# A two-layer graph network on one core: forward transforms by even and odd halves of the nodes on 64 by 64 tiles

## The chip, the core and the metric

The kernel runs on one core of a Trainium2 chip. The metric is the device time of one execution in microseconds (us); smaller is better. The engines are TensorE (PE in the profile, with PEld for its weight loads), VectorE (DVE), ScalarE (ACT), GpSimd (POOL) and SyncE (SP), which issues most of the DMAs. All data are fp32; an fp32 matmul appears in the trace as two records.

## The reference

The input holds 128 graphs of 128 nodes with 256 features. Layer 0 is a gated unit whose inputs are a convolution along the nodes and a message product; layer 1 is a graph convolution over five groups of nodes, cut here, since the change leaves it alone.

```python
h = relu(layernorm(x))                               # (128, 128, 256)
# layer 0, on h seen as 16 sequences of 2048 nodes elsewhere; here by graph
c = relu(bn1(conv1(h)))                              # 256 -> 256, one tap
c = bn2(conv2(c))                                    # 256 -> 256, 17 taps along the nodes, padding 8
x_conv = relu(c + h)
s = h @ w_se.T + b_se
A = exp(-dist(s)) * adj
x_nmp = A @ relu(h @ w_msg.T + b_msg)
z, r, n = gates([x_conv, x_nmp] @ w_ih.T, h @ w_hh.T)
x = x + (1 - z) * n + z * h
# layer 1
x = x + fused_graph_convs(relu(layernorm(x)))
```

conv2 is the part that matters here. Its 17 taps run along the 128 nodes of each graph.

## The kernel before

conv2 is computed in the frequency domain. With padding a graph's row of nodes has length 136 (LW), which gives 68 frequency pairs (NP_). Three stages follow one another.

**Heads.** The 128 graphs are worked in 32 blocks of four (BB). For each block: `head_load` fetches x by node (L196 on, tile ln), `head_stats` takes mean and variance on DVE (L204, L205, L208) and their power of -0.5 on POOL (L210), `head_norm` normalises on DVE (L223; the first blocks on ACT, L220), `head_turn` transposes on PE (L233) into two banks of PSUM, one for each half c of the features, and ACT writes them out with a relu (L234, tile ht), which SP stores to DRAM (htd, L235) for the gates. `head_conv1` multiplies by conv1's weights (L247), two graphs in a bank; DVE adds the shift of the batch norm (L250, tile h) and ACT takes the relu in place (`head_relu`, L254). `head_spectra` transforms along the nodes: for each half c and two graphs, a bank receives two matmuls with the 128 by 136 matrix fd (L263). The first two graphs' bank is copied to the spectra X by ACT (L273), the other's by DVE (L271), so the two engines read different banks. X is held in two tiles, X0 with 20 frequency pairs and X1 with 48, so each copy is two instructions of 80 and 192 columns.

Between these, `weight_spectra` (L176) transforms conv2's taps: four row tiles of 17 rows each write four banks; three of them are copied by ACT (L185), the fourth by DVE (L183), in two parts of the taps of three columns and a last of two that ACT copies alone. Each finished piece goes to DRAM (vd). Their operands w2 are loaded three buffers deep.

The engines keep the order in which the program is written in this stage. `heads` runs over i: conv1 of block i, first half; a piece of weight spectra; the relu; half of the statistics of block i+3; conv1, second half; the turn of block i+1; the relu; the norm of block i+2; on odd i another piece of weight spectra; the transforms of block i-1; the other half of the statistics. The work of one odd and one even i is called a pair of blocks below.

PSUM has eight banks, and `bank()` hands them out in a fixed cycle, each as a tile of its own:

```python
banks[1] = (n + 1) % 8
return pool.tile([P, 512], F32, tag=f"bank{n}", name="bank")
```

**Spectral products.** `spectral` takes one frequency pair after another: it loads the weight spectra v (four pairs at a time, SP), forms s = -2a - d on DVE (L334) from the two parts a and d of X, forms vs = vr + vi on POOL (L337, two instructions), multiplies by three groups of four matmuls (L340, L345), copies one product by ACT (L342), adds it on DVE (L346) and stores the result y.

**Gates and layer 1.** `load_h` loads ht again for each block, the inverse transform brings y back to nodes, and the message product, the gates and the second layer follow. The constants of the transforms are made on the host in `_spectral_constants`.

Of the kernel before, what the change touches and what calls it, by code (L numbers as in the profile page):

```python
# [75 lines left out]
def gnn_kernel(ctx: ExitStack, tc: tile.TileContext, io, out0: bass.AP, out1: bass.AP):  # L76
# [11 lines left out]
    turns = ExitStack()  # L88
    banks = [turns.enter_context(tc.tile_pool(name="turns", bufs=1, space=bass.MemoryType.PSUM)), 0]

    def bank():
        pool, n = banks
        if n is None:
            return pool.tile([P, 512], F32, tag="bank", name="bank")
        banks[1] = (n + 1) % 8
        return pool.tile([P, 512], F32, tag=f"bank{n}", name="bank")

# [6 lines left out]
    vec = cst.tile([P, NV], F32)  # L104
    fd = hc.tile([P, LW], F32)
    wc1 = hc.tile([P, C, D], F32)
# [6 lines left out]
    bnr = hc.tile([P, 2, D], F32)  # L113
    sh1 = bnr[:, 1, :]
    brz = cst.tile([P, 4], F32)

    def constant_loads():
        nc.sync.dma_start(wc1, io["wc1"].rearrange("(c p) o -> p c o", p=P))
        nc.sync.dma_start(fd, io["fd"])

    def constants():


        def scales(j, v0):
            g, b, m, v = (vec[:, v0 + 2 * q:v0 + 2 * q + 2] for q in range(4))
            sc, sh = bn[:, j, 0, :], bn[:, j, 1, :]
            ve = cst.tile([P, C], F32, name=f"bnve{j}")
            nc.vector.tensor_scalar(ve, v, EPS, None, op0=ALU.add)
            rs = cst.tile([P, C], F32, name=f"bnrs{j}")
            nc.gpsimd.tensor_tensor(rs, ve, mhalf[:, :C], op=ALU.pow)  # L130
            nc.vector.tensor_mul(sc, g, rs)
            nc.vector.tensor_mul(ve, m, sc)
            nc.vector.tensor_sub(sh, b, ve)

        scales(0, V_BN1)
        bnb = hc.tile([P, 2 * C, P], F32, name="bnb")
# [52 lines left out]

    xs, stats, hcs, h1s = {}, {}, {}, {}  # L190

# [20 lines left out]

    def head_norm(i, wk=None):
        mv, rs = stats.pop(i)
# [22 lines left out]

    def head_conv1(wk, i, h):
        if not h:
            h1s[i] = wk.tile([P, BB, D], F32, tag="h1", name="h1", bufs=2)  # L240
        ht = hcs[i]
        ps = bank()
        pv = ps.rearrange("p (b d) -> p b d", b=2)
        for bb in range(2):
            b = 2 * h + bb
            for c in range(C):
                nc.tensor.matmul(pv[:, bb, :], ht[:, c, b * N:(b + 1) * N], wc1[:, c, :],  # L247
                                 start=c == 0, stop=c == C - 1)
        hv = h1s[i][:, 2 * h:2 * h + 2, :]
        nc.vector.tensor_tensor(hv, pv, sh1[:, None, :].to_broadcast([P, 2, D]), op=ALU.add)  # L250

    def head_relu(i, h):
        hv = h1s[i][:, 2 * h:2 * h + 2, :]
        nc.scalar.activation(hv, hv, AF.Relu)  # L254

    def head_spectra(X, i):
        h1 = h1s.pop(i)
        g0 = i * BB
        for c in range(C):
            for h in range(BB // 2):  # L260
                ps = bank()
                for bb in range(2):
                    nc.tensor.matmul(ps[:, bb * LW:(bb + 1) * LW], h1[:, 2 * h + bb, c * P:(c + 1) * P], fd,  # L263
                                     start=True, stop=True)
                s = ps[:, :2 * LW].rearrange("p (g d) -> p d g", g=2)
                d0 = 0
                for xt in X:
                    xv = xt[:, c].rearrange("p a k g -> p (a k) g")
                    dst, d1 = xv[:, :, g0 + 2 * h:g0 + 2 * h + 2], d0 + 2 * xt.shape[2]
                    if h:  # L270
                        nc.vector.tensor_copy(dst, s[:, d0:d1])  # L271
                    else:
                        nc.scalar.copy(dst, s[:, d0:d1])  # L273
                    d0 = d1

    def heads(wk, xk, ahead, X, between, consts):

        for i in range(NBLK + 1):
            if i + ahead < NBLK:
                head_load(xk, ahead, i + ahead, nc.sync)  # L280
            if i < NBLK:
                head_conv1(wk, i, 0)
            between()
            if i < NBLK:
                head_relu(i, 0)
            if i == 0:
# [7 lines left out]
            if i < NBLK:  # L294
                head_relu(i, 1)
# [15 lines left out]
    def spectral(bp, X, p_from, p_to, amid):  # L311

        x, base = X
        for p in range(p_from, p_to):
# [66 lines left out]
    with front as es:  # L381
# [9 lines left out]
        with ExitStack() as ws:  # L391
# [20 lines left out]
            def some_spectra(k=1):  # L412
                for _ in range(k):
                    if not spectra and todo:
                        spectra.append(weight_spectra(wp, *todo.pop(0), taps.pop(0)))
                    if spectra and next(spectra[0], STOP) is STOP:
                        spectra.pop(0)
                        if len(todo) > 2:
                            taps.append(taps_load(wp, *todo[2], nc.sync))
                        some_spectra()  # L420
# [6 lines left out]
            nc.sync.dma_start(fw, row("fw", 5))  # L427
            taps.append(taps_load(wp, *todo[2], nc.sync))
            consts = constants()
            head_stats(hk, 0)  # L430
# [11 lines left out]
            some_spectra()  # L442
            heads(hk, xk, ahead, X, some_spectra, consts)
            while spectra or todo:
                some_spectra()
        turns.close()
        banks[:] = [ctx.enter_context(tc.tile_pool(name="psum", bufs=8, space=bass.MemoryType.PSUM, reuse_waits="tile")), None]

# [697 lines left out]


def _spectral_constants():

# [4 lines left out]
    def rows(t):  # L1154

        t = np.asarray(t)
        c = np.cos(2 * np.pi * np.outer(np.arange(NP_ + 1), t) / LW)
        s = np.sin(2 * np.pi * np.outer(np.arange(NP_ + 1), t) / LW)
        return c, s

    gt = np.zeros((P, NP_, 2))
    fd = np.zeros((P, NP_, 2))
    inv = np.zeros((NP_, 2, P))
    c, s = rows(np.arange(KW))
    for r in range(4):
        k = slice(32 * r, 32 * r + KW)
        gt[k, 0, 0], gt[k, 0, 1] = c[0], c[NP_]
        gt[k, 1:, 0], gt[k, 1:, 1] = c[f].T, s[f].T
    c, s = rows(np.arange(P) + PAD)
    fd[:, 0, 0], fd[:, 0, 1] = c[0], c[NP_]  # L1170
    fd[:, 1:, 0], fd[:, 1:, 1] = c[f].T, (-s[f] - c[f]).T
    c, s = rows(np.arange(P))
    inv[0, 0], inv[0, 1] = c[0] / LW, c[NP_] / LW
# [5 lines left out]
    d = {"gt": gt.reshape(P, LW), "fd": fd.reshape(P, LW), "idm": inv[:P], "idr": idr.reshape(P, 2 * P)}  # L1179
    return {k: np.ascontiguousarray(v, dtype=np.float32) for k, v in d.items()}  # L1180


def _lay_out(a):
# [10 lines left out]
    by = (-1, BB, P)  # L1194
    d = {"x": cc(a["x"].reshape(*by, 2 * P).transpose(0, 2, 1, 3)), "xT": cc(a["x"].reshape(-1, BB * P, 2, P).transpose(0, 3, 2, 1)), "adjT": cc(a["adj"].reshape(*by, P).transpose(0, 3, 1, 2))}
    d["vec"] = cc(np.concatenate(
# [72 lines left out]
```

## Time and profile before

| | us |
|---|---|
| median of three runs | 1842.88 (1842.33 to 1843.74) |
| the profiled execution, its own time | 1843.16 |
| its span in the trace | 1841.2 |
| heads (to the last PE work before the products) | 0 to 259.7 |
| spectral products | 262.8 to 437 |
| gates and layer 1 | 437 to the end |

The profile is of one execution. A line of a group names the source line, the engine, the operation, output and inputs with shapes and count, and after the bar the busy time, the mean duration in ns and the idle time of the engine ahead of these instructions with what ended it. The chain of waits is the sequence of work that ended last, followed back from the end. The table of windows gives busy time of each engine in a stretch; the granted clock is a share of full speed, and DMA the mean busy share of the 16 DMA engines.

### The profile page before, as it was taken

Reading aid. Unit: us, or ns where it says so; the run is one execution under the profiler, and the core shown is the slowest. Engines: PE = TensorE matmul, PEld = TensorE weight load, DVE = VectorE, ACT = ScalarE, POOL = GpSimd, SP = SyncE. Lnnn points to the kernel's source line nnn. Section 1 sums busy time; section 2 is a strip of 40 time slices with the busy share of each in tenths; the row PEclk is TensorE's granted clock in tenths of the full one; section 3 lists DMA queues with packets and bytes.
Section 4 is the critical chain, followed back from the end, with each engine's and each line's share of the span. In section 5 each row is a group of like instructions: output and inputs, shape, how many; then the busy total and the mean of one; then the engine's idle time right before and its main releaser. Section 6 shows DMA issues by size and latency. Waiting matters only on the chain.

```text
span 1841.2 us, 31324 instructions
## 1 busy us (share of the span) xinstructions
PE 1823.7 (99%) x11016; PEld 1587.0 (86%) x11016; DVE 1323.1 (72%) x3290; ACT 736.9 (40%) x1630; POOL 648.5 (35%) x803
## 2 busy tenths in 40 slices
PE   9999999999999999999999999999999999999998
PEld 7888888887888888888788888888788888888786
DVE  6888855556887887878665788878656677877553
ACT  6666641112443343333334433433343433343343
POOL 1111125675435443544221354344313234443100
PEclk9999999999999999999999999999999999999999
DMA  8888889996633333334234433333333533242134
GB/s 303 319 315 317 306 293 309 351 322 227 170 76 84 73 90 83 85 77 115 71 103 110 123 85 76 78 82 111 88 83 89 135 80 92 73 97 58 35 91 130
DMA packets 217904, 267.26 MB, mean 145 GB/s; under 512 B 104822, under 2 KB 181323, under 8 KB 215699
## 3 DMA queue, kind: packets, MB, share of 16 engines
q1 hardware_dynamic: 212563, 247.32, 45.2%
q10 hardware_dynamic: 5184, 17.93, 2.4%
q8 instruction: 88, 1.44, 0.3%
q14 instruction: 69, 0.57, 0.1%
HBM read 168.84 MB, written 96.35 MB: 144 GB/s over the span
## 4 chain that ended last, share of the span: by engine, by line
PE 92%; DMA 3%; DVE 2%; SPq 1%; POOL 1%; ACT 1%; issue 0%; DVEq 0%; POOLq 0%; ACTq 0%
PE bank L686 44%; PE bank L345 6%; PE bank L247 6%; PE bank L1013 5%; PE bank L954 5%; PE bank L587 5%; PE bank L340 3%; PE bank L263 3%; PE bank L637 3%; PE bank L566 3%; PE bank L176 2%; PE bank L233 1%; PE bank L933 1%; PE bank L863 1%; DMA nt<-in_adjN_dram 1%; PE bank L543 1%
## 5 line engine op out<-in xcount | busy, mean ns | idle before, releaser
L686 PE MATMUL bank<-t,sw 128*128 128x256 f32 x1152 | 291.8, 380 | 1.0 <-POOL t L661 0.4
L699 POOL TENSOR_TENSOR u<-u,m 128x256 f32<-128x256 f32 x128 | 93.7, 732 | 462.6 <-ACT m L697 413.9
L686 PEld LDWEIGHTS bank<-t,sw 128*128 128x128 f32 x1152 | 214.7, 190 | 34.0 <-issue 3.0
L686 PE MATMUL bank<-t,wih 128*128 128x256 f32 x768 | 200.2, 383 | 0.0
L686 PEld LDWEIGHTS bank<-t,wih 128*128 128x128 f32 x768 | 143.1, 190 | 29.3 <-DVE o L726 6.6
L337 POOL TENSOR_TENSOR vs<-v 128x256 f32<-128x256 f32 x134 | 98.7, 762 | 72.4 <-DMA v<-vd 48.6
L247 PE MATMUL bank<-wc,ht 128*128 128x256 f32 x512 | 124.0, 386 | 0.0
L686 PE MATMUL bank<-xc,wih 128*128 128x256 f32 x384 | 115.4, 382 | 1.6 <-ACT xc L570 1.6
L686 PE MATMUL bank<-xn,wih 128*128 128x256 f32 x384 | 115.1, 382 | 0.0
L686 PE MATMUL bank<-t,whh 128*128 128x256 f32 x384 | 114.6, 380 | 0.1
L1013 PE MATMUL bank<-w,hh 128*125 128x256 f32 (+9 forms) x480 | 113.6, 380 | 0.1
L686 PE MATMUL bank<-ht,whh 128*128 128x256 f32 x384 | 110.5, 381 | 0.5 <-DVE msg L606 0.4
L610 ACT ACTIVATE msg<-msg 128x512 f32<-128x512 f32 x64 | 36.8, 622 | 183.1 <-DVE msg L606 183.1
L570 ACT ACTIVATE xc<-xc,bn 128x512 f32<-128x512 f32 x64 | 46.2, 722 | 152.1 <-DVE xc L569 152.1
L210 POOL TENSOR_TENSOR rs<-ve,mhalf 128x4 f32<-128x4 f32 x32 | 32.3, 1009 | 207.5 <-DVE ve L208 201.2
L247 PEld LDWEIGHTS bank<-wc,ht 128*128 128x128 f32 x512 | 92.4, 190 | 14.2
L1013 PEld LDWEIGHTS bank<-w,hh 128*125 128x125 f32 (+9 forms) x480 | 84.4, 178 | 18.1 <-DVE hh L959 1.2
L185 ACT COPY sp<-bank 128x408 f32<-128x408 f32 (+1 forms) x160 | 66.8, 509 | 71.6 <-PE bank L176 71.6
L954 PE MATMUL bank<-ax,w 128*128 128x500 f32 (+9 forms) x352 | 94.4, 404 | 1.1 <-DVE xc L569 1.1
L334 DVE SCALAR_TENSOR_TENSOR s<-X 128x256 f32<-128x256 f32 x67 | 44.0, 659 | 66.4 <-PE bank L345 66.4
L704 DVE TENSOR_TENSOR u<-bank,u 128x256 f32<-128x256 f32 x128 | 53.4, 417 | 49.2 <-PE bank L686 48.6
L342 ACT COPY k<-bank 128x256 f32<-128x256 f32 x67 | 25.0, 373 | 145.9 <-PE bank L340 145.9
(214 smaller groups left out, 4423.8 us busy)
## 6 DMA issues: line engine op xcount, KB each, us to landing
vd<-sp SPq DMA_DIRECT2D x16, 2176.0 KB
v<-vd SPq DMA_DIRECT2D x34, 1024.0 KB
w<-in_w_dram SPq DMA_DIRECT2D x40, 512.0 KB
ln<-in_x_dram SPq DMA_DIRECT2D x32, 512.0 KB
htd<-ht SPq DMA_DIRECT2D x32, 512.0 KB
yd<-ys ACTq DMA_DIRECT2D x32, 512.0 KB
ht<-htd SPq DMA_DIRECT2D x32, 512.0 KB
ym<-yd SPq DMA_DIRECT2D x32, 512.0 KB
```

The costliest lines, as they stand in the source:

```text
L185: nc.scalar.copy(dst, s)
L247: nc.tensor.matmul(pv[:, bb, :], ht[:, c, b * N:(b + 1) * N], wc1[:, c, :], start=c == 0, stop=c == C - 1)
L263: nc.tensor.matmul(ps[:, bb * LW:(bb + 1) * LW], h1[:, 2 * h + bb, c * P:(c + 1) * P], fd, start=True, stop=True)
L337: nc.gpsimd.tensor_tensor(vs[:, c], vr[c], vi[c], op=ALU.add)
L340: nc.tensor.matmul(p1[:, :D], a[:, c], vs[:, c], start=c == 0, stop=c == C - 1)
L345: nc.tensor.matmul(ps[:, k * D:(k + 1) * D], u[:, c], w[c], start=c == 0, stop=c == C - 1)
L566: nc.tensor.matmul(ps[:, b * N:(b + 1) * N], ym[:, 2 * h + b, o * P:(o + 1) * P], idm, start=False, stop=b == 1)
L587: nc.tensor.matmul(ps[:, b, :], d[:, b * N:(b + 1) * N], w, start=True, stop=True)
L686: nc.tensor.matmul(ps, w, d, start=n == 0, stop=n == len(pairs) - 1)
L699: nc.gpsimd.tensor_tensor(got["u4"], got["u2"], got["m5"], op=ALU.add)
L954: nc.tensor.matmul(pv[:, q - q0, :], w1s[k5 + g][:, c, q * P:(q + 1) * P], xv[:, c], start=c == 0, stop=c == C - 1)
L1013: nc.tensor.matmul(ps[:n1, :D], hh[:, q, at:at + n1], w2s[k5 + g][:, q, :], start=q == 0, stop=q == HID // P - 1)
```

## The change

Nodes are put in an order in which the second 64 are mirrored: `_order()` reverses them, on the host, in x, in both dimensions of adj, and in the output. A block of x is laid out so that a tile's partitions hold the first halves of two graphs and its neighbour the mirrored second halves. Sum and difference of a node and its mirror then suffice: cosines act on the sums, sines on the differences, each with 64 nodes and 68 frequencies. `fd` becomes three 68-column parts: cosines, sines, and the sums of the cosines.

In the heads:

- `head_conv1` writes h = max(conv1, -shift) on DVE in place of the add, and the relu on ACT goes; the shift enters again as a constant (`shk`) when the spectra are written.
- `head_sums` forms sum and difference of the two halves on POOL, two instructions of 256 columns for each half of a block.
- `head_spectra` issues, for each half c of the features, 16 matmuls of 64 by 64 by 68 on four tiles into two banks; the two row tiles (one graph each) write one bank each; ACT copies the odd parts and DVE adds `shk` to the even parts, each of them from both banks, again in 80 and 192 columns.
- `bank()` hands out two-bank tiles; a bank is one half of such a tile.
- The norm of block i+2 is three instructions on ACT and one on POOL in place of four on DVE.
- On even i the transforms of block i-1 stand right behind the weight spectra, ahead of conv1's second half; on odd i they stay where they were.

In the products DVE forms s = d - a and d = d + a as two operations in place of one, POOL subtracts in place of adding. `load_h` puts ht back in the order of graphs by two DMAs in place of one. w2 has two buffers, `bnb` moves to another pool, and the constants of the inverse transform change on the host, not in size.

```diff
@@ bank
-        banks[1] = (n + 1) % 8
-        return pool.tile([P, 512], F32, tag=f"bank{n}", name="bank")
+        if n % 2 == 0:
+            two = pool.tile([P, 2, 512], F32, tag=f"bank{n // 2}", name="bank")
+        banks[1:] = (n + 1) % 8, two
+        return two[:, n % 2, :]
+
+    def two_banks():
+        if banks[1] % 2:
+            bank()
+        bank(), bank()
+        return banks[2]
@@ constants
+        for c in range(C):
+            nc.gpsimd.tensor_scalar(shk[:, c, :], fd[:, 2, :], bn[:, 0, 1, c:c + 1], -2.0, op0=ALU.mult, op1=ALU.mult)
@@ taps_load
-        w2 = pool.tile([P, WCH // 4, P], F32, tag="w2", name="w2", bufs=3)
+        w2 = pool.tile([P, WCH // 4, P], F32, tag="w2", name="w2", bufs=2)
@@ head_norm
-            if wk is not None:
+            if wk is not None and (b < BB - 1 or last is None):
                 nc.scalar.activation(xs[i][:, b, :], xs[i][:, b, :], AF.Identity, bias=nm[:, b:b + 1],
                                      scale=rs[:, b:b + 1])
                 continue
-            nc.vector.tensor_scalar(xs[i][:, b, :], xs[i][:, b, :], mv[:, b, 0:1], rs[:, b:b + 1],
-                                    op0=ALU.subtract, op1=ALU.mult)
+            (last or nc.vector).tensor_scalar(xs[i][:, b, :], xs[i][:, b, :], mv[:, b, 0:1], rs[:, b:b + 1],
+                                              op0=ALU.subtract, op1=ALU.mult)
@@ head_conv1, head_relu, head_sums
-        nc.vector.tensor_tensor(hv, pv, sh1[:, None, :].to_broadcast([P, 2, D]), op=ALU.add)
-
-    def head_relu(i, h):
-        hv = h1s[i][:, 2 * h:2 * h + 2, :]
-        nc.scalar.activation(hv, hv, AF.Relu)
+        nc.vector.tensor_tensor(hv, pv, nsh1[:, None, :].to_broadcast([P, 2, D]), op=ALU.max)
+
+    def head_sums(ep, i, h):
+        if not h:
+            evens[i] = ep.tile([P, 2, D], F32, tag="ev", name="ev", bufs=2)
+        lo, hi = h1s[i][:, 2 * h, :], h1s[i][:, 2 * h + 1, :]
+        nc.gpsimd.tensor_tensor(evens[i][:, h, :], hi, lo, op=ALU.add)
+        nc.gpsimd.tensor_tensor(hi, hi, lo, op=ALU.subtract)
@@ head_spectra
         for c in range(C):
+            ps = two_banks()
             for h in range(BB // 2):
-                ps = bank()
-                for bb in range(2):
-                    nc.tensor.matmul(ps[:, bb * LW:(bb + 1) * LW], h1[:, 2 * h + bb, c * P:(c + 1) * P], fd,
-                                     start=True, stop=True)
-                s = ps[:, :2 * LW].rearrange("p (g d) -> p d g", g=2)
-                d0 = 0
-                for xt in X:
-                    xv = xt[:, c].rearrange("p a k g -> p (a k) g")
-                    dst, d1 = xv[:, :, g0 + 2 * h:g0 + 2 * h + 2], d0 + 2 * xt.shape[2]
-                    if h:
-                        nc.vector.tensor_copy(dst, s[:, d0:d1])
-                    else:
-                        nc.scalar.copy(dst, s[:, d0:d1])
-                    d0 = d1
+                for e in range(2):
+                    c0 = (2 * h + e) * NP_
+                    u = h1[:, 2 * h + 1, :] if e else ev[:, h, :]
+                    for bb in range(2):
+                        r = slice(64 * bb, 64 * bb + 64)
+                        for q in range(2):
+                            o = c * P + 64 * q
+                            nc.tensor.matmul(ps[64 * q:64 * q + 64, bb, c0:c0 + NP_], u[r, o:o + 64], fd[r, e, :],
+                                             start=True, stop=True)
+            sv = ps[:, :, :4 * NP_].rearrange("p b (h e k) -> p e k h b", h=2, e=2)
+            d0 = 0
+            for xt in X:
+                n = xt.shape[2]
+                to = xt[:, c, :, :, g].rearrange("p k e (h b) -> p e k h b", h=2)
+                nc.scalar.copy(to[:, 1], sv[:, 1, d0:d0 + n])
+                nc.vector.tensor_tensor(to[:, 0], sv[:, 0, d0:d0 + n],
+                                        shk[:, c, d0:d0 + n, None, None].to_broadcast([P, n, 2, 2]), op=ALU.add)
+                d0 += n
@@ heads
             between()
+            if i and i % 2 == 0:
+                head_spectra(X, i - 1)
...
             elif i + 2 < NBLK:
-                head_norm(i + 2)
+                head_norm(i + 2, wk, nc.gpsimd)
...
-            if i > 0:
+            if i % 2:
                 head_spectra(X, i - 1)
@@ spectral
-            nc.vector.scalar_tensor_tensor(s, a, -2.0, d, op0=ALU.mult, op1=ALU.subtract)
+            nc.vector.tensor_tensor(s, d, a, op=ALU.subtract)
+            nc.vector.tensor_tensor(d, d, a, op=ALU.add)
...
-                nc.gpsimd.tensor_tensor(vs[:, c], vr[c], vi[c], op=ALU.add)
+                nc.gpsimd.tensor_tensor(vs[:, c], vi[c], vr[c], op=ALU.subtract)
@@ load_h
-        nc.sync.dma_start(ht, htd[i])
+        to = ht.rearrange("p c (b s j) -> p s (c b) j", s=2, j=N // 2)
+        of = htd[i].rearrange("p c (h s b j) -> p s (c h) b j", s=2, b=2, j=N // 2)
+        for k in range(2):
+            nc.sync.dma_start(to[:, k].rearrange("p (h b) j -> p h b j", b=2), of[:, k])
```

More of the change, by code (lines that the diff above doesn't have):

```diff
@@ L88, in gnn_kernel @@
     turns = ExitStack()
-    banks = [turns.enter_context(tc.tile_pool(name="turns", bufs=1, space=bass.MemoryType.PSUM)), 0]
+    banks = [turns.enter_context(tc.tile_pool(name="turns", bufs=1, space=bass.MemoryType.PSUM)), 0, None]
     def bank():
-        pool, n = banks
+        pool, n, two = banks
         if n is None:
             return pool.tile([P, 512], F32, tag="bank", name="bank")
-        banks[1] = (n + 1) % 8
-        return pool.tile([P, 512], F32, tag=f"bank{n}", name="bank")
+        if n % 2 == 0:
[7 more added lines that the diff above has]
+        return banks[2]
     def row(name, n):
@@ L104, in gnn_kernel @@
     vec = cst.tile([P, NV], F32)
-    fd = hc.tile([P, LW], F32)
+    fd = hc.tile([P, 3, NP_], F32)
+    shk = hc.tile([P, C, NP_], F32)
     wc1 = hc.tile([P, C, D], F32)
@@ L113, in gnn_kernel @@
     bnr = hc.tile([P, 2, D], F32)
-    sh1 = bnr[:, 1, :]
+    nsh1 = bnr[:, 1, :]
     brz = cst.tile([P, 4], F32)
@@ L118, in constant_loads, with constants @@
         nc.sync.dma_start(wc1, io["wc1"].rearrange("(c p) o -> p c o", p=P))
-        nc.sync.dma_start(fd, io["fd"])
-    def constants():
+        nc.sync.dma_start(fd.rearrange("p e k -> p (e k)"), io["fd"])
+    def constants(pool):
         def scales(j, v0):
@@ L132, in scales @@
             nc.vector.tensor_mul(ve, m, sc)
-            nc.vector.tensor_sub(sh, b, ve)
+            if j:
+                nc.vector.tensor_sub(sh, b, ve)
+            else:
+                nc.vector.tensor_sub(sh, ve, b)
         scales(0, V_BN1)
-        bnb = hc.tile([P, 2 * C, P], F32, name="bnb")
+        bnb = pool.tile([P, 2 * C, P], F32, tag="ev", name="bnb", bufs=2)
         nc.scalar.copy(bnb, bn[:, 0].rearrange("p q c -> p (q c)")[:, :, None].to_broadcast([P, 2 * C, P]))
@@ L187, in weight_spectra @@
         nc.sync.dma_start(vd[c, q], sp)
-    xs, stats, hcs, h1s = {}, {}, {}, {}
+    xs, stats, hcs, h1s, evens = ({} for _ in range(5))
     def head_load(pool, ahead, i, queue):
@@ L211, in head_stats, with head_norm @@
                 stats[i] = mv, rs
-    def head_norm(i, wk=None):
+    def head_norm(i, wk=None, last=None):
         mv, rs = stats.pop(i)
@@ L242, in head_conv1 @@
         ps = bank()
-        pv = ps.rearrange("p (b d) -> p b d", b=2)
-        for bb in range(2):
-            b = 2 * h + bb
+        pv = ps.rearrange("p (s d) -> p s d", s=2)
+        for s in range(2):
             for c in range(C):
-                nc.tensor.matmul(pv[:, bb, :], ht[:, c, b * N:(b + 1) * N], wc1[:, c, :],
+                nc.tensor.matmul(pv[:, s, :], ht[:, c, (2 * h + s) * N:(2 * h + s + 1) * N], wc1[:, c, :],
                                  start=c == 0, stop=c == C - 1)
@@ L256, in head_spectra @@
     def head_spectra(X, i):
-        h1 = h1s.pop(i)
-        g0 = i * BB
+        h1, ev = h1s.pop(i), evens.pop(i)
+        g = slice(i * BB, (i + 1) * BB)
         for c in range(C):
+            ps = two_banks()
             for h in range(BB // 2):
-                ps = bank()
-                for bb in range(2):
-                    nc.tensor.matmul(ps[:, bb * LW:(bb + 1) * LW], h1[:, 2 * h + bb, c * P:(c + 1) * P], fd,
-                                     start=True, stop=True)
-                s = ps[:, :2 * LW].rearrange("p (g d) -> p d g", g=2)
-                d0 = 0
-                for xt in X:
-                    xv = xt[:, c].rearrange("p a k g -> p (a k) g")
-                    dst, d1 = xv[:, :, g0 + 2 * h:g0 + 2 * h + 2], d0 + 2 * xt.shape[2]
-                    if h:
-                        nc.vector.tensor_copy(dst, s[:, d0:d1])
-                    else:
-                        nc.scalar.copy(dst, s[:, d0:d1])
-                    d0 = d1
@@ L276, in heads @@
-    def heads(wk, xk, ahead, X, between, consts):
+                for e in range(2):
[7 more added lines that the diff above has]
+                                             start=True, stop=True)
@@ L278, in heads @@
+    def heads(wk, xk, ep, ahead, X, between, consts):
         for i in range(NBLK + 1):
@@ L283, in heads @@
             between()
+            if i and i % 2 == 0:
+                head_spectra(X, i - 1)
             if i < NBLK:
-                head_relu(i, 0)
+                head_sums(ep, i, 0)
             if i == 0:
@@ L294, in heads @@
             if i < NBLK:
-                head_relu(i, 1)
+                head_sums(ep, i, 1)
             if i == 0:
@@ L417, in some_spectra @@
                         spectra.pop(0)
-                        if len(todo) > 2:
-                            taps.append(taps_load(wp, *todo[2], nc.sync))
+                        if len(todo) > 1:
+                            taps.append(taps_load(wp, *todo[1], nc.sync))
                         some_spectra()
@@ L427, in gnn_kernel @@
             nc.sync.dma_start(fw, row("fw", 5))
-            taps.append(taps_load(wp, *todo[2], nc.sync))
-            consts = constants()
+            consts = constants(wp)
             head_stats(hk, 0)
@@ L442, in gnn_kernel @@
             some_spectra()
-            heads(hk, xk, ahead, X, some_spectra, consts)
+            heads(hk, xk, wp, ahead, X, some_spectra, consts)
             while spectra or todo:
@@ L446, in gnn_kernel @@
         turns.close()
-        banks[:] = [ctx.enter_context(tc.tile_pool(name="psum", bufs=8, space=bass.MemoryType.PSUM, reuse_waits="tile")), None]
+        banks[:] = [ctx.enter_context(tc.tile_pool(name="psum", bufs=8, space=bass.MemoryType.PSUM, reuse_waits="tile")), None, None]
         bp = es.enter_context(tc.tile_pool(name="bp", bufs=1, reuse_waits="tile"))
@@ L1145, in gnn_kernel, with _order @@
         pass
+def _order():
+    import numpy as np
+    return np.concatenate([np.arange(P // 2), np.arange(P // 2)[::-1] + P // 2])
 def _spectral_constants():
@@ L1154, in rows @@
     def rows(t):
[L1156 to L1159, printed above, removed]
+        w = 2 * np.pi * np.outer(np.arange(NP_ + 1), np.asarray(t)) / LW
+        return np.cos(w), np.sin(w)
     gt = np.zeros((P, NP_, 2))
-    fd = np.zeros((P, NP_, 2))
+    fd = np.zeros((P, 3, NP_))
     inv = np.zeros((NP_, 2, P))
-    c, s = rows(np.arange(KW))
+    c, s = rows(np.arange(KW) - PAD)
     for r in range(4):
@@ L1167, in _spectral_constants @@
         gt[k, 0, 0], gt[k, 0, 1] = c[0], c[NP_]
[L1168 to L1173, printed above, removed]
+        gt[k, 1:, 0], gt[k, 1:, 1] = -c[f].T, s[f].T
+    c, s = rows((P - 1) / 2 - np.arange(P // 2))
+    for r in range(2):
+        k = slice(64 * r, 64 * r + 64)
+        fd[k, 0] = c[:NP_].T
+        fd[k, 1, 0], fd[k, 1, 1:] = s[NP_], s[f].T
+        fd[k, 2] = c[:NP_].sum(1)
+    c, s = rows(_order() - (P - 1) / 2)
+    inv[0, 0], inv[0, 1] = c[0] / LW, s[NP_] / LW
     inv[1:, 0], inv[1:, 1] = 2 * c[f] / LW, -2 * s[f] / LW
@@ L1178, in _spectral_constants @@
         idr[:, b * NR:(b + 1) * NR, b] = inv[P:]
-    d = {"gt": gt.reshape(P, LW), "fd": fd.reshape(P, LW), "idm": inv[:P], "idr": idr.reshape(P, 2 * P)}
+    d = {"gt": gt.reshape(P, LW), "fd": fd.reshape(P, 3 * NP_), "idm": inv[:P], "idr": idr.reshape(P, 2 * P)}
     return {k: np.ascontiguousarray(v, dtype=np.float32) for k, v in d.items()}
@@ L1194, in _lay_out @@
     by = (-1, BB, P)
-    d = {"x": cc(a["x"].reshape(*by, 2 * P).transpose(0, 2, 1, 3)), "xT": cc(a["x"].reshape(-1, BB * P, 2, P).transpose(0, 3, 2, 1)), "adjT": cc(a["adj"].reshape(*by, P).transpose(0, 3, 1, 2))}
+    n = _order()
+    x, adj = a["x"][:, n], a["adj"][:, n][:, :, n]
+    d = {"x": cc(x.reshape(-1, BB // 2, 2, 2, P // 2, 2 * P).transpose(0, 2, 4, 1, 3, 5).reshape(-1, P, BB, 2 * P)),
+         "xT": cc(x.reshape(-1, BB * P, 2, P).transpose(0, 3, 2, 1)),
+         "adjT": cc(adj.reshape(*by, P).transpose(0, 3, 1, 2))}
     d["vec"] = cc(np.concatenate(
@@ L1266 @@
     r = run_bass_kernel_spmd(nc, [arrays], core_ids=[0]).results[0]
-    return np.concatenate([r["out_1_dram"].transpose(2, 3, 1, 0).reshape(b, NN, ch),
-                           r["out_0_dram"].transpose(0, 3, 4, 2, 1).reshape(b, n - NN, ch)], axis=1)
+    out = np.empty((b, n, ch), np.float32)
+    out[:, _order()] = np.concatenate([r["out_1_dram"].transpose(2, 3, 1, 0).reshape(b, NN, ch),
+                                       r["out_0_dram"].transpose(0, 3, 4, 2, 1).reshape(b, n - NN, ch)], axis=1)
+    return out
```

## The prediction

> **What bounds the kernel now.** First the page: how busy each engine is, then the chain that ended last.
>
> ```profile
> PE 1823.7 (99%) x11016; PEld 1587.0 (86%) x11016; DVE 1323.1 (72%) x3290; ACT 736.9 (40%) x1630; POOL 648.5 (35%) x803
> PE 92%; DMA 3%; DVE 2%; SPq 1%; POOL 1%; ACT 1%; issue 0%; DVEq 0%; POOLq 0%; ACTq 0%
> ```
>
> TensorE (PE) sets the time nearly everywhere. Next the table of windows: the second row holds eight steady pairs of blocks of the heads, the stage that the change rewrites, the third the spectral products.
>
> ```profile
> 91.07:214.64 123.57, 123.57 (x1154) 107.18 (x1153) 101.38 (x320) 77.85 (x209) 16.13 (x16) 1.00 0.84 316
> 256.00:437.00 181.00, 179.58 (x847) 157.93 (x846) 92.22 (x142) 27.70 (x77) 116.80 (x158) 1.00 0.92 315
> ```
>
> The columns are PE, PEld, DVE, ACT, POOL, clock, DMA share, GB/s. In the heads PE never pauses; DVE has 22.2 us spare of 123.57, ACT 45.7, POOL nearly all. Then the chain inside one pair (odd block, then even):
>
> ```profile
> 91.07 2.05 PE bank L263 x16
> 93.12 1.73 PE bank L247 x8
> 94.85 0.91 PE bank L176 x24
> ...
> 105.61 0.91 PE bank L176 x24
> 106.52 2.05 PE bank L263 x16
> ```
>
> A pair takes 106.52 - 91.07 = 15.45 us, all PE. Last the durations, from the groups of that window:
>
> ```profile
> L263 PE MATMUL bank<-fd,h 128*128 128x136 f32 x257 | 33.5, 283 | 0.0
> L204 DVE BATCH_NORM_STATS2 st<-ln 128x6 f32<-128x256 f32 x64 | 26.0, 406 | 7.8 <-DMA ln<-in_x_dram 7.8
> L250 DVE TENSOR_TENSOR h<-bank,bnr 128x512 f32<-128x512 f32 x32 | 22.0, 687 | 2.8 <-PE bank L247 1.5
> L234 ACT ACTIVATE ht<-bank 128x512 f32<-128x512 f32 x32 | 17.4, 594 | 7.2 <-PE bank L233 7.2
> L273 ACT COPY X<-bank 128x192 f32<-128x192 f32 x32 | 11.6, 387 | 0.0
> L271 DVE COPY X<-bank 128x192 f32<-128x192 f32 x32 | 11.4, 355 | 0.0
> ```
>
> The idle column of L250 shows what matters: before, no engine waits long for another, since a bank comes round after seven others.
>
> **What the Trainium skill says.** "TensorEngine Tiling (Array Packing)", Key Properties: tiles work independently, but a change of tiling mode drains TensorE. The trace agrees: by the starts of single records L176's four row tiles go in waves of four, 6.7 ns apart, one wave per 116 ns, and a change into or out of L176 costs about 0.2 us. "PSUM — Partial Sum Buffer", PSUM bank collisions: "Semaphore-guard PSUM by **bank × quadrant** (by bank is the simple version), not by address." Guards of more than one bank are thus a choice of the program; before has one bank per tile. "SBUF — State Buffer", two separate sides: a DVE operation with two SBUF inputs and a GpSimd operation lock each other out. The trace has L334 (two SBUF inputs, in the spectral products) at 424 ns alone and 870 ns beside POOL, while L346 (one input in PSUM) stays at 691.
>
> **The change, part by part.** Per pair of blocks unless said; before and after by lines of the respective kernel.
>
> *Matmuls.* L263 issues 32 records per pair 116 ns apart: 3.71 us. New L287: 128 records of half the columns on four tiles. If a wave of four takes half of L176's 116 (as many columns halve the time there: 256 columns take 216 ns, 136 take 116), 32 waves x 0.059 = 1.89: -1.81. If the weights of two column tiles queue, a wave takes 118 and the gain is nil; I take -1.81. L287 has a tile layout of its own, so a pair has eight changes of layout, not six: +0.42.
>
> *Elementwise work.* ACT loses four relus (L254, 0.64) and gains six norms (0.61); DVE loses eight norms (0.41), gains little; POOL gains eight sums and two norms, ten of some 0.73 (L699), beside two powers of 1.0: some 9.3 of 15.45. None reaches PE's time, so this is nothing by itself (its cover is PE's 15.45). POOL's sums add a link, DVE's maximum to the transforms, some 1.5 us, but the transforms follow a block later; bound: 0 to 0.9 in the last blocks.
>
> *Banks in pairs: where I put the loss.* A tile now spans two banks and waits follow the tile. The compiled order with its waits, row numbers ahead, has in each steady pair (L261 is conv1, L247 the turn, L190 the weight spectra, L264 conv1's maximum on DVE, L248 the turn's relu on ACT):
>
> ```
> 568 L261 bank_2237 (conv1)   570 L190 bank_2237 [waits DVE]
> 593 L261 bank_2312 (conv1)   595 L247 bank_2312 [waits DVE]
> 598 L247 bank_2324 (turn)    600 L261 bank_2324 [waits ACT]
> 613 L247 bank_2390 (turn)    615 L190 bank_2390 [waits ACT]
> ```
>
> So PE fills one half, and may write the other only when the first has been emptied, by an instruction issued that moment. Behind PE's waiting matmul stands all its work, and DVE and ACT wait in turn for that.
>  (a) Turn to next (600, 615): ACT's first evacuation starts 0.63 us after the turn (four transposes and their latency), the second 0.49 later and lasts 0.60, so it ends at 1.72; PE is done at 0.87 (the chain's L233 x8) and goes on at 1.78: 0.91, twice: 1.82.
>  (b) conv1 to turn where DVE is free (after the odd block): last record start + matmul 0.38 + L264 0.04 + 0.69 + 0.05 = 1.16, less 0.21 that the record takes anyway: 0.96.
>  (c) conv1 to L190 (570), behind transforms: ACT and DVE each read from both of L287's banks, one tile, and the orders of ACT and DVE show that X's copy on ACT and its sum on DVE now wait for each other: ACT 80 columns, DVE 80, ACT 192, DVE 192, for two c. With 0.26 + 0.24 + 0.39 + 0.36, hand-offs of 0.05 and the two c overlapping by one step that is 2.4 us, where before the two engines read different banks at once. From the start of L190's 24 records at 0: ACT's three spectra copies (0.41 apart) end at 2.64, the ping-pong at 4.93; two stats with aggregates and L222, which stand ahead of L264 on DVE (2 x (0.41 + 0.18) + 0.15), at 6.26, L264 at 6.91. PE has done L190 (0.91), 16 waves (0.95), conv1 (1.73) and the layout changes and small waits between by 4.53 and goes on at 6.96: 2.43.
>  (d) the same at the second L190 and turn (595): DVE's L264 ends at 13.14, PE is ready at 11.01: 2.18 with hand-off.
>  (e) smaller waits on ACT's spectra copies: 0.92.
> Sum 1.82 + 0.96 + 2.43 + 2.18 + 0.92 = 8.31. Laying out before's order in the same way gives 15.39 for 15.45 measured, so the method holds where nothing waits.
>
> *Pair:* 15.45 - 1.81 + 0.42 + 8.31 = 22.37, +6.92. Fifteen such pairs: +104. Blocks 0 and 31 and the last store of vd (7.49 in the chain, then v's load 9.36) keep their chain, I add +1.
>
> *Spectral products.* Per frequency DVE has two operations with two SBUF inputs for one: 2 x 0.87 beside POOL + 0.69 = 2.43, below PE's 2.59 (12 matmuls of 0.216). Nothing if they fit; if DVE's order delays s, up to 0.2 x 67 = 13.
>
> *Loads.* The h load in two DMAs of 256-byte runs: SP issues 32 more, each fetched two blocks ahead. w2 with two buffers instead of three: some 11 us from issue to landing against 13 to its use; a longer period gives more. Both nothing, at worst 2.
>
> Own time 1843.16 (span 1841.2 + 1.96) + 105 = 1948. The median of the runs, 1842.88, is 0.3 below, so 1948 stands for it too.
>
> **The rivals.**
>  1. *Only hand-offs count* (1892): the ping-pong and stats come earlier than I laid them out, so (c) and (d) shrink to the 0.95 of (b). Waits 1.82 + 3 x 0.95 = 4.67, pair 18.7, +3.3 x 15 = +49. For: 0.05 per hand-off and all of DVE's order are laid out from single durations. Against: ACT has three copies ahead, whose 0.41 is measured.
>  2. *Column tiles queue* (1975): waves of 118 ns take back the 1.81, 27 in all, little of it beneath the waits, as X's copies wait for the transforms. For: no trace here has column tiles. Against: L176's row tiles do overlap.
>  3. *Pairs cost nothing, faster* (1822): a wait that the order shows is met because ACT and DVE run ahead of PE. Then a pair is 15.45 - 1.39 = 14.06, x 15 = -21. It decides as soon as the waits per pair sum to less than 1.39 us. For: ACT and DVE have much spare time. Against: each of the waits is for a read of what PE wrote last, so no spare time helps; (a) and (b) alone are 2.8.
>  4. *Waits and gain cancel*: needs the sum at 1.39; nothing speaks for it.
>
> **How the numbers follow.** Forecast as above 0.60, rival 1 0.19, rival 2 0.13, rival 3 0.06, rival 4 0.02. The likeliest's own range, from hand-offs of 0.03 to 0.08 and stats shorter or longer, is 1920 to 1975. The range 1885 to 1988 takes in rivals 1 and 2 with the bounds above (spectral 13) and leaves out rival 3 and the tails. About 0.2% (3.7 us) is what a measurement can tell from no change: faster 0.06, same 0.02, slower 0.92.
>
> **What would show it.** In after's window of steady pairs PE's busy share should fall to some two thirds, with idle time before L190 and L247 (released by DVE's L264) and before L261 and L190 (released by ACT's L248); a pair of 22.4 us; L287's waves 59 ns apart; the start of the spectral products at some 368 us, not 262.8; their pace of 2.59 unchanged, and the gates to the end 1404 us as before. A pair under 14 us, or no idle PE there, makes the forecast wrong; waves of 118 ns speak for rival 2; idle PE only of 0.9 each for rival 1; a longer stage after the heads for something I have not seen.

## The result, and the profile after

The changed kernel takes 1960.66 us (four runs, 1953.54 to 1963.28) against 1842.86 (1842.33 to 1843.74): ratio 1.0633, 95% interval 1.0605 to 1.0661. It is slower by 118 us, 13 more than forecast. The profiled execution took 1960.83, its span is 1959.0.

Page of the profile after, busy time of each engine and the share of each engine in the chain that ended last:

```profile
PE 1851.1 (94%) x12552; PEld 1585.2 (81%) x12552; DVE 1335.6 (68%) x3270; ACT 751.4 (38%) x1653; POOL 778.7 (40%) x962
PE 84%; DVE 5%; ACT 5%; issue 2%; DMA 1%; POOL 1%; SPq 1%; ACTq 0%; DVEq 0%; POOLq 0%
```

PE is no longer busy throughout, and the chain has moved partly onto DVE and ACT. The table of windows says where (PE, PEld, DVE, ACT, POOL, clock, DMA share, GB/s):

```profile
296.00:318.00 22.00, 15.42 (x244) 11.87 (x240) 10.77 (x34) 10.88 (x30) 10.22 (x12) 1.00 0.60 222
120.00:142.00 22.00, 18.81 (x236) 14.89 (x237) 9.22 (x29) 11.13 (x28) 9.70 (x12) 0.74 0.53 196
551.00:1955.00 1404.00, 1397.44 (x7897) 1217.18 (x7896) 1034.06 (x2513) 549.21 (x1137) 496.56 (x605) 1.00 0.37 94
```

The first row is one steady pair of blocks: PE busy 15.42 of 22.00 us, and no engine over half full except PE. The second lies earlier in the heads: the granted clock is 0.74, and PE is busier only because its matmuls last longer. The third is gates and layer 1, as full of PE as before.

What PE waited for in 150 us of the heads (waits of PE; time, times, longest):

```profile
PE bank L190 <- DVE h L264: 10.5, 6, 1.9
PE bank L247 <- DVE h L264: 9.0, 7, 1.7
PE bank L247 <- issue: 5.8, 7, 0.8
PE bank L261 <- ACT ht L248: 5.5, 7, 0.8
PE bank L190 <- ACT ht L248: 5.5, 7, 0.8
PE bank L287 <- ACT sp L199: 1.4, 6, 0.2
```

Seven times in the window stands for once in a pair. These are the places named in the prediction; the third, put down to "issue", is the turn after the odd block's conv1: L264 is issued as soon as conv1's bank is full (in one pair it runs from 314.48 to 315.17) and ends just before the turn starts at 315.27, so it is wait (b). The view counts idle time from the modelled end of the matmul before, so each is some 0.2 us less than from start to start (a record of L261 is drawn 0.38 long, while such records start 0.22 apart). The chain of waits inside one pair, from conv1's maximum to conv1 behind the turn:

```profile
301.02 0.60 DVE h L264
...
301.66 0.97 PE bank L190 x23
302.66 1.60 ACT sp L199 x3
304.25 0.10 ACT X L294
...
304.38 0.25 DVE X L295
304.65 0.33 ACT X L294
...
305.01 0.52 DVE X L295 x2
...
306.25 0.35 DVE st L218
...
307.33 0.59 DVE h L264
...
307.96 0.67 PE bank L247 x4
...
308.71 0.41 ACT ht L248
...
309.20 0.60 ACT ht L248
...
309.85 1.99 PE bank L261 x8
```

PE's own part in the 6.9 us from the first maximum to the turn is 0.97. ACT and DVE hand the transforms' banks to and fro, then DVE does the statistics, then the maximum, and only then may the turn write the other half of that pair of banks. Behind the turn the same happens with ACT: conv1 starts only when ACT has read both of the turn's banks.

### The profile page after: what moved, and what is told of

Its sections match the earlier page's. It is cut to its first block, busy times and chain, and to the rows that moved or that the text cites. A ratio compares the mean times of both kernels' runs of the same rounds, so it can differ in the third digit from the quotient of the medians.

```text
span 1959.0 us, 34582 instructions
## 1 busy us (share of the span) xinstructions
PE 1851.1 (94%) x12552; PEld 1585.2 (81%) x12552; DVE 1335.6 (68%) x3270; ACT 751.4 (38%) x1653; POOL 778.7 (40%) x962
## 4 chain that ended last, share of the span: by engine, by line
PE 84%; DVE 5%; ACT 5%; issue 2%; DMA 1%; POOL 1%; SPq 1%; ACTq 0%; DVEq 0%; POOLq 0%
PE bank L714 42%; PE bank L371 6%; PE bank L1041 5%; PE bank L615 5%; PE bank L982 5%; PE bank L261 4%; PE bank L366 3%; PE bank L665 3%; PE bank L594 3%; PE bank L190 1%; PE bank L961 1%; ACT sp L199 1%; DVE X L295 1%; PE bank L891 1%; ACT ht L248 1%
## 5 line engine op out<-in xcount | busy, mean ns | idle before, releaser
L714 PEld LDWEIGHTS bank<-t,sw 128*128 128x128 f32 x1152 | 214.6, 190 | 33.4 <-issue 2.8
L261 PE MATMUL bank<-wc,ht 128*128 128x256 f32 x512 | 145.7, 434 | 17.5 <-ACT ht L248 11.8
L261 PEld LDWEIGHTS bank<-wc,ht 128*128 128x128 f32 x512 | 104.2, 214 | 41.9 <-ACT ht L248 15.4
L1041 PEld LDWEIGHTS bank<-w,hh 128*125 128x125 f32 (+9 forms) x480 | 85.4, 180 | 18.7 <-DVE hh L987 1.2
L270 POOL TENSOR_TENSOR ev<-h 128x256 f32<-128x256 f32 x64 | 46.5, 727 | 115.0 <-DVE nm L231 86.7
L264 DVE TENSOR_TENSOR h<-bank,bnr 128x512 f32<-128x512 f32 x64 | 43.9, 686 | 64.2 <-PE bank L261 59.1
L190 PE MATMUL bank<-gt,w 17*128 17x136 f32 x1024 | 47.3, 306 | 39.0 <-DVE h L264 28.0
```

What stands on the lines that cost most here:

```text
L190: nc.tensor.matmul(ps[r][:, j * LW:(j + 1) * LW], w2[32 * r:32 * r + KW, s0 + j, :], gt[32 * r:32 * r + KW, :], start=True, stop=True)
L261: nc.tensor.matmul(pv[:, s, :], ht[:, c, (2 * h + s) * N:(2 * h + s + 1) * N], wc1[:, c, :], start=c == 0, stop=c == C - 1)
L714: nc.tensor.matmul(ps, w, d, start=n == 0, stop=n == len(pairs) - 1)
L1041: nc.tensor.matmul(ps[:n1, :D], hh[:, q, at:at + n1], w2s[k5 + g][:, q, :], start=q == 0, stop=q == HID // P - 1)
```

## The experiments

Each ratio is to the kernel before as it was measured on the same chip beside that run: its median was 1842.86 us for the change, 1846.41 for the first four runs behind it and 1847.07 for the last two. Runs of different groups are therefore compared by their ratios.

| run | us | ratio, 95% interval | pair of blocks, us |
|---|---|---|---|
| change | 1960.66 | 1.0633 (1.0605 to 1.0661) | 22.0 |
| single banks | 1851.61 | 1.0032 (1.0018 to 1.0047) | 15.8 |
| pairs alone | 2102.06 | 1.1407 (1.1352 to 1.1462) | 27.4 to 34.9 |
| statistics behind | 1949.22 | 1.0559 (1.0510 to 1.0608) | 20.8 |
| single banks, old order | 1846.88 | 0.9997 (0.9986 to 1.0009) | 15.3 |
| the same, norm late on ACT | 1834.30 | 0.9933 (0.9919 to 0.9946) | 14.2 to 15.2 |
| banks in pairs, old order | 2053.33 | 1.1118 (1.1097 to 1.1140) | 27.6 to 33.4 |

The pair is the distance of the starts of every second group of transforms in the trace; a single number is the commonest one, and single pairs lie above it.

**Single banks.** One part of the change undone:

```diff
-        if n % 2 == 0:
-            two = pool.tile([P, 2, 512], F32, tag=f"bank{n // 2}", name="bank")
-        banks[1:] = (n + 1) % 8, two
-        return two[:, n % 2, :]
+        banks[1] = (n + 1) % 8
+        return pool.tile([P, 512], F32, tag=f"bank{n}", name="bank")
...
-            ps = two_banks()
+            ps = [bank(), bank()]
...
+            for b in range(2):
...
+                    nc.scalar.copy(to[:, 1, b], sv[b][:, 1, d0:d0 + n])
+                    nc.vector.tensor_tensor(to[:, 0, 1 - b], sv[1 - b][:, 0, d0:d0 + n],
+                                            shk[:, c, d0:d0 + n, None].to_broadcast([P, n, 2]), op=ALU.add)
```

> The changed kernel with every bank a tile of its own; the transforms' two banks are read bank by bank, ACT taking the odd parts of one while DVE takes the even parts of the other, then the reverse. Everything else stays. Theory (waits that follow the two-bank tile make the loss): conv1 to weight spectra, conv1 to turn and turn to weight spectra stop waiting, the pair of blocks falls from 22.0 us to some 15.7 (what stays: conv1 waits 0.4 for ht after the turn, since it needs the data, 0.7 for ACT's spectra copies and the transforms 0.9 for the DVE maximum), the time to 1845 to 1860. Rival (the loss comes from the work itself that moved to ACT and POOL, or from the 64 by 64 tiles): pair stays above 20 us, time above 1930.

Measured: 1851.61, pair 4.63 + 11.16 = 15.79. The theory's pair and time hold, the rival is out. What PE still waits for in 123 us, over eight pairs (lines of this kernel: L253 conv1, L191 ACT's copies of the weight spectra, L240 ht, L279 the transforms, L256 the maximum):

```profile
PE bank L253 <- ACT sp L191: 5.2, 8, 0.9
PE bank L253 <- ACT ht L240: 2.1, 7, 0.3
PE bank L279 <- DVE h L256: 1.6, 8, 0.2
```

Weight spectra and turn no longer wait at all. Conv1 behind the turn still waits 0.3 for ht: it needs the data, so of that 0.8 only 0.5 belonged to the banks. The transforms wait 0.2 where 0.9 was laid out. What is left here, some 1.1 us a pair in this view, is thus not due to banks in pairs. This run undoes the pairs and the alternation at once, since both come from the same tile; their shares were not separated.

**Pairs alone.** The converse, the kernel before with the two-bank `bank()` and nothing else (the lines cut only carry a third entry of `banks`):

```diff
...
-        banks[1] = (n + 1) % 8
-        return pool.tile([P, 512], F32, tag=f"bank{n}", name="bank")
+        if n % 2 == 0:
+            two = pool.tile([P, 2, 512], F32, tag=f"bank{n // 2}", name="bank")
+        banks[1:] = (n + 1) % 8, two
+        return two[:, n % 2, :]
...
```

> The kernel before with one thing of the change: the bank handed out is half of a two-bank tile. Theory: PE waits for the evacuation of what it wrote last, and the X copies of ACT and DVE alternate; laid out with the measured durations the pair goes from 15.45 us to some 25.8, the time to 1990 to 2015, more than the whole change. Rival (a pair of banks by itself costs only the hand-offs, about 1 us each at four places): pair 19, time 1890 to 1900. Rival (no cost): 1843.

Measured: 2102.06, above the theory by some 90. The direction is right and the loss larger than the whole change's; the size is not. PE's waits in 123 us (L265 the transforms, L275 ACT's copies of X, L178 the weight spectra, L252 conv1's sum, L235 the turn, L236 ht), and its window:

```profile
PE bank L265 <- ACT X L275: 12.7, 16, 1.2
PE bank L178 <- DVE h L252: 6.4, 8, 0.8
PE bank L235 <- ACT ht L236: 5.5, 8, 0.7
```

```profile
91.00:214.00 123.00, 89.94 (x577) 69.64 (x576) 51.05 (x161) 40.33 (x104) 8.06 (x8) 0.81 0.43 158
```

The places are those that the order shows. What was not laid out is the clock, the third number from the end: 0.81. No whole pair is free of half clock: those that meet it for 3.4 us take 27.4, 1.6 more than laid out, and of those that meet it for 10 to 24 us all but one take 29.7 to 34.9.

**Statistics behind.** The change with the statistics moved to where DVE is free:

```diff
-            elif i + 3 < NBLK:
-                head_stats(wk, i + 3, (0,))
             if i < NBLK:
                 head_conv1(wk, i, 1)
+            if i and i + 3 < NBLK:
+                head_stats(wk, i + 3)
...
-            if i + 3 < NBLK:
-                head_stats(wk, i + 3, (1,) if i else (0, 1))
+            if i == 0:
+                head_stats(wk, 3)
```

> The changed kernel with both halves of the statistics moved behind conv1's second half, so that on DVE no statistics stand between the sums of the spectra and the maximum that PE waits for. Theory: (c) and (d) of the prediction are made of the ping-pong and of the statistics behind it. Laid out again with the measured durations, the whole falls by 21 us, not by the 37 that the 1.33 + 1.17 us per pair would give: 1935 to 1945. Rival (the statistics cost nothing, only the ping-pong and the hand-offs count): 1960.

Measured: 1949.22, with runs from 1940.34 to 1962.07, and an interval that just touches that of the change; by the time alone the gain is not sure, and the median lies 4 us above the theory's range. The trace is clearer: the pair is 20.8 against 22.0, and PE's waits in the same 150 us are

```profile
PE bank L190 <- DVE h L264: 6.0, 7, 0.9
...
PE bank L287 <- ACT sp L199: 5.8, 7, 1.0
...
PE bank L247 <- DVE h L264: 5.5, 7, 0.8
```

The two waits for the maximum fall from 1.9 and 1.7 to 0.9 and 0.8, the bare hand-off, as the theory has it. A good part comes back as a new wait: the transforms now wait 0.8 for ACT's spectra copies instead of 0.2, because ACT does its norms late, behind the statistics that now stand ahead of `nm` on DVE. In the profiled executions the first product comes at 358.2 us instead of 378.8, near the 21 us laid out, but half clock is part of that: 30 us of it in the heads instead of 61.

**Single banks, old order.** Single banks as above, and:

```diff
-            if i and i % 2 == 0:
-                head_spectra(X, i - 1)
...
-                head_norm(i + 2, wk, nc.gpsimd)
+                head_norm(i + 2)
...
-            if i % 2:
+            if i > 0:
                 head_spectra(X, i - 1)
```

> Single banks as in the first run of this call, and besides the transforms of even blocks back behind the turn and the norm back on DVE as before; the even and odd halves, the sums on POOL and the maximum stay. Theory: PE stops nowhere in a steady pair; it keeps the matmuls' gain and pays the layout changes, pair 14.1 us, and the time falls below both kernels to 1820 to 1830. Rival (64 by 64 tiles don't pay once the layout changes are counted, or DVE becomes the limit with norm, statistics and sums): 1843 or more.

Measured: 1846.88, no difference from before. A miss: the rival is right, and of its two causes it is DVE's limit, as the next run shows. The window of the heads and DVE's norm in it:

```profile
91.00:214.50 123.50, 119.95 (x1922) 99.16 (x1921) 116.52 (x386) 69.01 (x240) 63.70 (x81) 1.00 0.86 317
```

```profile
L229 DVE TENSOR_SCALAR ln<-ln,mv,rs 128x256 f32<-128x256 f32 x64 | 37.0, 638 | 0.0
```

DVE is busy 116.52 of 123.50. Its norm, 406 ns before, takes 638 in the mean here and up to 885. POOL, 16 us busy in such a window before, is busy 63.7. The trace ties the two together: of the 64 norms in the window 28 took 399 to 406 ns, none of them beside POOL's work for more than 0.4 us, and 36 took 589 to 885, each beside POOL's work for some 0.6 us or more. That the two keep each other from SBUF would explain it; that is only argued. The layout took 406.

**Norm late on ACT.** The run before with the norm on ACT and POOL again, but behind the transforms' copies:

```diff
-            elif i + 2 < NBLK:
-                head_norm(i + 2)
...
+            if i and i + 2 < NBLK:
+                head_norm(i + 2, wk, nc.gpsimd)
             if i + 3 < NBLK:
                 head_stats(wk, i + 3, (1,) if i else (0, 1))
```

> Single banks, the transforms of even blocks behind the turn, and the norm on ACT and POOL as in the change but issued behind the copies of the spectra and of X. In the run with the norm on DVE that stage was DVE's: its norm took 638 ns instead of 406 beside POOL's sums, DVE was busy 116.5 of 123.5 us. Theory: with six of the eight norms of a pair on ACT (busy some 12 of 14 us) no engine reaches PE, the pair is 14.2 us by the order laid out, and the time 1824 to 1830. Rival (the loads set the pace: the heads already move 317 GB/s and the products no more than 318): pair no less than 14.9, time 1836 to 1842. Rival (ACT is too full and PE waits for its copies): pair above 15, time 1845 or more.

Measured: 1834.30, ratio 0.9933: 0.7% faster than the kernel before, between theory and first rival. The quickest pair takes 14.21 us (6.80 + 7.41), as laid out, most take 14.3 to 14.9, the longest 15.2. The window, and what DVE's statistics (L210) waited for in it:

```profile
91.00:214.50 123.50, 121.97 (x2029) 101.05 (x2028) 91.09 (x356) 98.64 (x304) 87.04 (x102) 1.00 0.90 333
```

```profile
DVE st L210 <- DMA ln<-in_x_dram: 15.5, 8, 2.5
```

PE waits only 1.3 us in all in this window, but the loads of x come late by up to 2.5 us, at a DMA share of 0.90 and 333 GB/s; before it was 0.84 and 316. The loads are on the chain in this stage (five of some 11 to 12 us). Whether the loads account for the rest was not tried.

**Banks in pairs, old order.** The change with the transforms of even blocks back in their place:

```diff
-            if i and i % 2 == 0:
-                head_spectra(X, i - 1)
...
-            if i % 2:
+            if i > 0:
                 head_spectra(X, i - 1)
```

> The changed kernel, banks in pairs, with only the transforms of even blocks put back behind the turn. Theory (waits by the pair meet whatever stands ahead in the order of DVE and ACT): ACT's spectra copies now stand behind the transforms' ping-pong and PE meets it at more places; laid out with the measured durations the pair is 25.7 us against 22.3 laid out for the change, the time 2000 to 2025. Rival (the new place of the transforms is part of the loss, as conv1 then waits for ht 0.9 us): a pair of some 21, time 1945.

Measured: 2053.33, above the theory's range, and the rival is out: the new place of the transforms gains some 90 us (ratio 1.0633 against 1.1118) as long as banks come in pairs. The wait of PE that stands out in 123 us:

```profile
PE bank L190 <- DVE h L264: 21.6, 9, 3.0
```

The wait of the weight spectra for the maximum grows from 1.9 to 3.0 and comes in both blocks of a pair; the clock is 0.79 in that window. The quickest pair takes 27.6 where 25.7 was laid out, but each of these pairs meets some 10 us or more of half clock, so the two can't be told apart.

## Why the prediction was right, and where its sum was off

The stages first, in us, by the starts of the matmuls:

| stage | before | after | difference |
|---|---|---|---|
| to the first product | 259.7 | 378.8 | +119.1 |
| products | 177.2 | 177.0 | -0.2 |
| gates and layer 1 | 1404.4 | 1403.3 | -1.1 |

The 262.8 at which the products begin in the table of times before is not their first matmul: six records ran ahead of it, and then PE waited 1.36 us for v. The matmuls that come at 262.81 before come at 380.38 after, 12 later than the 368 of the prediction.

```profile
259.66 0.59 PE L329 MATMUL bank<-v,X 128*128 128x256 f32 x2
262.81 1.53 PE L329 MATMUL bank<-v,X 128*128 128x256 f32 x6 [1.36 <-DMA v<-vd]
```

```profile
378.76 0.67 PE L354 MATMUL bank<-v,X 128*128 128x256 f32 x2 [2.01 <-DVE X L295]
```

In the prediction's own table of windows two rows are shown, of which the first is the heads and the second the products. In (c) its own durations put the end of L264 at 6.26 + 0.69 = 6.95, not 6.91; that changes nothing.

- *Matmuls on four tiles, -1.81.* Right. Two waves of four records start 0.12 us after the two before them, which is 59 ns a wave, so the weights of the column tiles don't queue and rival 2 is out:

```profile
302.81 0.30 PE L287 MATMUL bank<-fd,h 64*64 64x68 f32 x8
302.93 0.30 PE L287 MATMUL bank<-fd,ev 64*64 64x68 f32 x8
```

  The quickest pair of the norm late on ACT takes 14.21 against the 14.06 that the prediction's gain and layout changes alone give.
- *Waits (a) to (e), 8.31.* Right in kind and nearly in size: a pair that meets no half clock takes 22.0, so the waits sum to 22.0 - 15.45 + 1.81 - 0.42 = 7.94. (a) is right in size (PE goes on 309.85 - 307.96 = 1.89 after the turn's start, for 1.78), but for conv1 behind the turn I gave the bank as the cause alone; the single-bank run leaves 0.3 of it to the data. (b) is 0.83 idle for 0.96. (c) and (d), 1.9 and 1.7 idle at the longest, and some 0.2 more from start to start, are less than 2.43 and 2.18: the ping-pong in the chain shown takes 2.00 (304.25 to 306.25) and not the 2.29 laid out (2.64 to 4.93), as ACT's copies of X took 244 and 318 ns, not 261 and 387. (e) is some 0.3 idle a pair for 0.92. Rival 1 is out, since it has a pair at 18.7 and no wait over 0.9 or so, and so is rival 3: the waits are met, and with the pairs gone they go.
- *Fifteen pairs, +104.* Thirteen whole pairs, from the transforms of block 1 to those of block 27, took 297.0 us against 200.9: +96.1. At 22.0 each it would have been +85; the other 11 fall on the pairs that meet half clock, which no step of the prediction has. The blocks ahead of them add 13.5 and those behind 9.5; for these 23, two pairs' worth, the sum had 2 x 6.92 + 1 = 14.8. Of the 9.5, 2.0 is a wait that the prediction doesn't name: the first product waits for DVE's last sum into X; 0.7 is PE's wait for POOL's sums, for which 0 to 0.9 was given. The rest of these ends was not taken apart. So the sum for the heads, 105, was short of 119 by 11 for the clock and 8 for the ends, less 5 for a pair laid out 0.36 too long; that the last hid part of the first two is luck.
- *Elementwise work, nothing by itself.* Not quite: with single banks in the order of the change a pair takes 15.8 and not 14.06. The 1.7 that stay are mostly PE's waits for ACT's copies of the weight spectra and for ht, and the run with the norm late on ACT and the old order, which has the same elementwise work, takes most of them away. POOL's part of the norm takes 1223 ns, not the 0.73 us that I took, without effect that these runs show. Moving the norm off DVE, which I counted as nothing, is worth something once the banks are single: some 12 us by the ratios of the fourth and the fifth run.
- *Products, nothing.* Right: -0.2, and their pace stays at 2.59 us. DVE fits, at 126.55 of 174 us busy. *Loads* nothing: right.

The deciding step was to read the waits of the compiled order, and to ask of each whether it is for the instruction issued just before. That DVE and ACT are idle half the time didn't help, as rival 3 would have it.

## What to carry to other kernels

Where the waits that a compiler sets follow the tile, as here, a PSUM tile of two banks halves the number of independent places: what is written second waits for whoever reads the first, and two engines that read disjoint parts take turns. Where the reading can be split between engines by bank, give each bank its own tile and let them swap; they still meet at the swap (in the run with single banks and the old order ACT waited up to 2.5 us there for DVE), so neither may come late to its half. When a kernel has no slack on TensorE, the price of such a wait is not the evacuation alone but everything that stands ahead of it in the reader's queue. And a layout made from durations at full clock leaves out what happens to the clock once TensorE idles: 11 us in thirteen pairs of the change, and more where banks come in pairs in the old order.

## What the runs showed of the hardware that was not expected

In the heads the granted clock fell to half in stretches of 3.41 us or a multiple of it. From 29 us on to the first product PE idled, by the trace, 0 to 9% of the time in the kernel before and in the three runs with single banks, and half clock came for 0 to 3.4 us. It idled 25% with the statistics moved (30 us at half clock), 26% in the change (61), 27% with pairs alone (183) and 32% with pairs in the old order (188). So idle time goes with it, but 25 and 26% gave 30 and 61 us; what exactly sets it off was not tried. Of the whole pairs of the change up to block 27 those without half clock took 22.0 us, those with a single stretch of 3.4 us mostly 22.3 to 22.4, those with two of them mostly 23.6 to 24.0.

DVE's norm, one SBUF input and one output, took 589 to 885 ns where it ran beside POOL's work for 0.6 us or more, and 399 to 406 elsewhere; in the same window the statistics (405, beside POOL or not) and conv1's maximum (671 against 687) were not slowed.
